# Routing to experts between the products of a graph network's last pass

## The chip, the cores and the metric

The program runs on one core of one Trainium2 chip. The metric is the device time of one execution in microseconds (us). Its engines have short names throughout: PE is TensorE's matmuls and PEld its weight loads, DVE is VectorE, ACT is ScalarE, POOL is GpSimd and SP is SyncE, which here only issues DMAs (SPq is its queue). Engines run their own instruction streams in order and wait for each other on semaphores.

## The reference, cut to what matters

The network has four layers over 3125 nodes of 256 features and 50000 edges. Each layer adds to `x` a graph part and a mixing part of the normed `x`, and then a feed-forward part. The change is in the fourth layer (number 3):

```python
xn = _layernorm(x)
x = x + gcn(xn, edges) + linear_attention(xn)      # gcn: three convolutions
# feed-forward of layer 3: 8 experts, each node goes to 2 of them
xt = _layernorm(x)
probs = softmax(xt @ Wr + br)
top_p, top_idx = top_k(probs, 2);  weights = top_p / top_p.sum(-1)
xe = norm(xt) * ln_g[e] + ln_b[e]                  # a second norm, affine by expert
y  = gelu(xe @ W1[e] + b1[e]) @ W2[e] + b2[e]      # 256 -> 1024 -> 256
x  = x + sum over the two experts of weights * y
```

One convolution is `agg[dst] += h[src] * norm`, then a bias. The third (512 to 256 features) ends with the sum over neighbours that finishes `x` for the feed-forward part.

## The kernel before, in words

**Tiles.** Nodes lie in `NB` = 25 blocks of 128 rows; `x` stays in SBUF. Where work goes by groups, a group is `BB` = 5 blocks. The program is written with a tile framework: Python calls record instructions, the framework gives tiles their buffers and every instruction its semaphore waits, and it may move an instruction that depends on nothing nearby to an earlier place. Pools are opened and closed; a tile in a pool opened later may lie where a closed pool lay, and then waits for that pool's readers.

**Layer 3's graph part.** `layer3` (L2294) reads a number and takes one of two branches of the program: `gcn3`, by gathers, or `dense3` (L2103), which this input takes. `dense3` does the sum over neighbours as a matrix product with a matrix of edge counts, one block of destinations at a time: `product(h, d)` (matmuls L2134) loads the 128 x 3200 bf16 counts of block `d` (0.8 MB, tile `a`, three buffers, by SP) and runs 75 matmuls of 128x256 (25 blocks of sources by three bf16 parts that make up an f32 value) into the PSUM tile `dn`, which has two buffers. Four passes of 25 products make the three convolutions (the second has 512 features, so two passes). In the last pass (L2219 to L2223) each product is followed by a single DVE instruction (L2222) that scales it and adds it to `x[:, d, :]`. When it has run for a block, that block of `x` is final for the feed-forward part. The PSUM pool of `dense3`, `ps`, has three buffers by default; besides `dn` it holds tiles called `mm`.

**The feed-forward part.** `ffn3` (L2305) calls `ffn` (L1726), which calls `mixture` (L1306), shared by layers 0, 1 and 3. `mixture` makes its tiles and returns two functions:

- `route(b)` (L1333 to L1395) for the group that starts at block `b`. Statistics of five blocks (`stats`, L435: on DVE the statistics L441 and L442 and the reciprocal L445, on ACT a square root L444), then for each block the norm on DVE (`normed`, L448), two transposes on PE and a copy out of PSUM on ACT or DVE (`to_T`, L451), and two matmuls per k for the 8 logits (`tok`, L459; an f32 matmul is two rows in the profile). Then a second norm into `xs`; the bias, the exponential, the softmax's division and the choice of two (`exps` L1543, `over_sum` L1553, `top2` L1565: DVE, with one ACT instruction). Two small matmuls over the group's choices count for each node how many earlier nodes went to the same expert; `run`, carried from group to group, adds the counts of earlier groups. DVE makes row numbers of them (L1368 and after), and POOL issues ten indirect DMAs (L1389) that scatter the five blocks of `xs` to `sent`, a DRAM table sorted by expert.
- `rest()` (L1397 to L1541) opens the pool of weights, loads `w2` of all experts (L1402, 8 issues of 1 MB by SP), works out on DVE which expert each of `ES` = 56 slots of 128 rows belongs to, and then runs the slots: for each SP loads the routed block `xr` (L1462), that expert's `w1` (L1464) and bias `br` (L1466); PE transposes and multiplies (`h`, L1494; `y`, L1507) with a Gelu on ACT between (L1498), and POOL scatters the result back (L1511). A last loop (L1538) adds both results of each node to `x`.

`ffn` calls `route` for the five groups one after the other, and then `rest`. All of this stands behind the join of the two branches. `mixture` also splits the experts' second bias `b2` into three bf16 parts and stores them in DRAM (`split3`, L1291: a load and a store by SP, five small instructions on DVE).

**What sets the order around the change.** Each engine runs in the order in which the framework placed the instructions, which is for the most part the order of the Python calls. In the last pass that is product after product; on SP, the loads of `a`, three products ahead at most. The branches of `layer3` are blocks of their own: nothing of the feed-forward part that uses `x` can stand ahead of the join.

Of the kernel before, what the change touches and what calls it, by code (L numbers as in the profile page):

```python
# [19 lines left out]
P = 128  # L20
N = 3125
D = 256
# [42 lines left out]
class Net:  # L65
# [484 lines left out]
    def gather_sum(self, pool, ps, table, w, agg, weighted=False, steps=None):  # L550
# [4 lines left out]
        for g in range(NS // G):  # L555
            msg = []
            for j in range(G):
                if j % n == 0:
                    m = pool.tile([P, n, w], F32, name="msg", bufs=7)
                self.gather(m[:, j % n, :], table, g * G + j)  # L560
                msg.append(m[:, j % n, :])
# [744 lines left out]
    def mixture(self, whole, mark, pre, names, kind, gate, gate_b, H, act, twice=False, affine=None):  # L1306


        nc, tc, a = self.nc, self.tc, self.a
# [10 lines left out]
        head = whole.enter_context(ExitStack())  # L1320
        r1 = head.enter_context(self.pool("ro", 1, side="right"))
        r = head.enter_context(self.pool("ro2", 2, side="right"))
        ps = head.enter_context(self.pool("ro_ps", 2, PSUM))

        xs = r1.tile([P, NB, DX], F32, name="xs")
        nc.vector.tensor_copy(xs[:, :, D:D + 2], self.goes)
        wg = self.weight(r1, gate)
        bg = self.rows(r1, gate_b[0])
        for nm in gate_b[1:]:
            nc.vector.tensor_add(bg, bg, self.rows(r1, nm))  # L1330
        b2d = self.split3(r, a[b2n].rearrange("e h -> (e h)"), NE * D, pre + "b2_3")

        def route(b):  # L1333
            mv, rs = self.stats(r, lambda i: self.x[:, b + i, :], BB, "ln")
            q = ps.tile([P, BB, NE], F32, name="lg", bufs=1)
            rows = xs[:, b:b + BB, :D]
            xn = r.tile([P, BB, D], F32, name="xn") if twice else rows
            for i in range(BB):
                self.normed(xn[:, i, :], self.x[:, b + i, :], mv, rs, i)
                xg = r.tile([P, 2, P], F32, name="xg", bufs=4)  # L1340
                self.to_T(ps, xn[:, i, :], xg)
                self.tok(q[:, i, :], xg, 0, wg)
# [15 lines left out]
            if kind != "plain":  # L1358
                self.over_sum(r, c, guard=b + BB == NB)

            q = ps.tile([P, 2, BB, NE], F32, name="rk", bufs=1)
# [24 lines left out]
            for i in range(BB):  # L1386
                n = LAST if b + i == NB - 1 else P
                for k in range(2):
# [4 lines left out]
                    if b + i + k:  # L1393
                        tc.declare_no_dep(s.ins, group=pre, reason="every row has a place of its own")
                    tc.add_to_no_dep_group(pre, s.ins)  # L1395

        def rest():  # L1397
# [3 lines left out]
            for e in range(NE):  # L1401
# [3 lines left out]
            w1d = a[w1n].rearrange("e d f -> (e d) f")  # L1405

            ni = r1.tile([P, NE], I32, name="ni")
            nc.vector.tensor_scalar(ni, run, 127.0, None, op0=ALU.add)
            nc.vector.tensor_scalar(ni, ni, 7, None, op0=ALU.logical_shift_right)
            nf = r1.tile([P, NE], F32, name="nf")  # L1410
            nc.vector.tensor_copy(nf, ni)
            zero = r1.tile([P, NE], F32, name="zero")
            nc.vector.memset(zero, 0.0)
            st = r1.tile([P, NE], F32, name="st")
            nc.vector.tensor_tensor_scan(st, nf, zero, 0.0, ALU.add, ALU.add)
            nc.vector.tensor_sub(st, st, nf)
            sl = r1.tile([1, ES], F32, name="sl")
            nc.gpsimd.iota(sl, pattern=[[1, ES]], base=0, channel_multiplier=0,  # L1418
                           allow_small_or_imprecise_dtypes=True)
            ex = r1.tile([1, ES], F32, name="exf")  # L1420
            nc.vector.memset(ex, 0.0)
            st0 = r1.tile([1, ES], F32, name="st0")
            nc.vector.memset(st0, 0.0)
            for e in range(1, NE):
                s = st[0:1, e:e + 1]
                nc.vector.scalar_tensor_tensor(ex, sl, s, ex, op0=ALU.is_ge, op1=ALU.add)
                t = r.tile([1, ES], F32, name="stt")
                nc.vector.tensor_scalar(t, sl, s, s, op0=ALU.is_ge, op1=ALU.mult)
                nc.vector.tensor_tensor(st0, st0, t, ALU.max)
            nc.vector.tensor_sub(sl, sl, st0)  # L1430

            place = r1.tile([1, ES], F32, name="place")
            nc.vector.tensor_scalar(place, sl, float(P), None, op0=ALU.mult)
            nc.vector.scalar_tensor_tensor(place, ex, float(NP), place, op0=ALU.mult, op1=ALU.add)
            q = ps.tile([P, ES], F32, name="own", bufs=1)
            nc.tensor.matmul(q, self.ones[0:1, :], place, start=True, stop=True)
            own, void = (p.tile([P, ES], F32, name=n) for n in ("own", "void"))
            nc.vector.tensor_scalar(own, q, self.row, float(1 + mark), op0=ALU.add, op1=ALU.add)
            nc.vector.tensor_scalar(void, q, self.row, float(2 * NP), op0=ALU.add, op1=ALU.add)
            nc.vector.tensor_scalar(sl, sl, float(NB - 1), float(P), op0=ALU.min, op1=ALU.mult)  # L1440
            exi = p.tile([1, ES], I32, name="exi")
            nc.vector.tensor_copy(exi, ex)
            rows_at = p.tile([1, ES], I32, name="rows_at")
            nc.vector.scalar_tensor_tensor(rows_at, ex, float(NP), sl, op0=ALU.mult, op1=ALU.add)
            head.close()
# [95 lines left out]
        return route, rest  # L1541
# [39 lines left out]
    def layer0(self):  # L1581
        with ExitStack() as whole:
            rest = []

            def after():
                route, r = self.mixture(whole, 0, "L0_ffn_", ("W1", "b1", "W2", "b2"), "plain", "L0_ffn_gate_w",
                                        ["L0_ffn_gate_b"], 512, AF.Gelu)
                rest.append(r)
                return route
# [15 lines left out]
            rest[0]()  # L1605
# [120 lines left out]
    def ffn(self, *args, **more):  # L1726
        with ExitStack() as whole:
            route, rest = self.mixture(whole, *args, **more)
            for b in range(0, NB, BB):
                route(b)  # L1730
            rest()

    def ffn1(self):
        self.ffn(1, "L1_ffn_", ("W1", "b1", "W2", "b2"), "chosen", "L1_ffn_Wg", ["L1_ffn_bg", "L1_ffn_bias"], 512, AF.Relu)
# [368 lines left out]
    def dense3(self):  # L2103
# [4 lines left out]
        with self.pool("dense", 1) as gw, self.pool("counted", 3) as ap, self.pool("dense2", 2) as gp, \  # L2108
# [69 lines left out]
            with self.pool("late", 1) as lw:  # L2178
# [33 lines left out]
                for half, h in enumerate((hb, ha)):  # L2212
                    for d in range(NB + 2):
# [4 lines left out]
                        if half and d >= 2 and ((d - 2) % 4 == 3 or d - 2 == NB - 1):  # L2218
                            wide((d - 2) // 4)  # L2219
                for d in range(NB):  # L2220
                    q = product(hb, d)
                    nc.vector.scalar_tensor_tensor(self.x[:, d, :], q, di[:, d:d + 1], self.x[:, d, :],  # L2222
                                                   op0=ALU.mult, op1=ALU.add)  # L2223

    def gcn3(self):
        nc, tc = self.nc, self.tc
        with self.pool("gnn", 1) as gw, self.pool("gnn2", 2) as gp:
# [18 lines left out]
            with self.pool("ps3", 2, PSUM) as ps, self.pool("mix", 1) as mw, \  # L2246
# [5 lines left out]
                self.gather_sum(gp, ps, tabs[0], D, half, steps=steps)  # L2252
# [11 lines left out]
                self.gather_sum(gp, ps, tabs[1], 512, agg, steps=steps)  # L2264
# [22 lines left out]
                self.gather_sum(gp, ps, tabs[2], D, half, steps=steps)  # L2287
# [6 lines left out]
    def layer3(self):  # L2294
        nc, tc = self.nc, self.tc
        unfit = nc.values_load(self.gathers[0:1, 0:1], min_val=0, max_val=3 * P,
                               skip_runtime_bounds_check_because="a count of rows, in three ways")
# [112 lines left out]
```

## Time and profile before

| what | value |
|---|---|
| time, median of 3 runs | 6230.42 us (6222.06 to 6235.17) |
| the profiled execution's own time | 6871.84 us |
| its span | 6870.1 us |
| mean granted clock of TensorE in it | 0.825 |
| busy in the span | PE 4752.5, DVE 3279.0, POOL 2383.8, ACT 1573.9 us |
| layer 3's last pass over destinations | 6067 to 6272 us |
| its routes | 6272 to 6400 us |
| its expert slots | from 6400 us to about 6830 us |

The profile is one execution on the chip; the hardware's profiler makes it longer than the executions that are timed, by 641 us here. Times inside it are given from the start of the span. PE is busiest, but no engine is busy all the time: the share of each is an average over many stages. In a row of the timeline the columns are the start, the duration, the engine with its source line, the operation, the tiles (written from read), the shapes, how many were put together, and in brackets how long the engine had been idle and what ended that. In the table by windows, PEclk is the mean clock that was granted to TensorE, as a share of full speed.

### The profile page before, as it was taken

Reading aid. Unit: us, or ns where it says so; the run is one execution under the profiler, and the core shown is the slowest. Engines: PE = TensorE matmul, PEld = TensorE weight load, DVE = VectorE, ACT = ScalarE, POOL = GpSimd, SP = SyncE. Lnnn points to the kernel's source line nnn. Section 1 sums busy time; section 2 is a strip of 40 time slices with the busy share of each in tenths; the row PEclk is TensorE's granted clock in tenths of the full one; section 3 lists DMA queues with packets and bytes.
Section 4 is the critical chain, followed back from the end, with each engine's and each line's share of the span. In section 5 each row is a group of like instructions: output and inputs, shape, how many; then the busy total and the mean of one; then the engine's idle time right before and its main releaser. Section 6 shows DMA issues by size and latency. Waiting matters only on the chain.

```text
span 6870.1 us, 81944 instructions
## 1 busy us (share of the span) xinstructions
PE 4752.5 (69%) x25310; PEld 3363.4 (49%) x25310; DVE 3279.0 (48%) x8628; ACT 1573.9 (23%) x4113; POOL 2383.8 (35%) x2340
## 2 busy tenths in 40 slices
PE   2375776396575556555577756777169999997797
PEld 1012344284454434433366313444046788786696
DVE  5146676634687537775534346667533200113222
ACT  1012223322100034442222112221124311101222
POOL 1605776321665534445231625665110000001211
PEclk9677888598787777777688877888589999997898
DMA  3362333264222223333155322333111232123454
GB/s 106 85 179 66 107 107 102 83 199 118 86 84 74 71 76 116 116 109 102 53 167 173 90 79 83 102 107 94 37 55 62 72 135 87 58 78 113 171 175 160
DMA packets 385094, 710.59 MB, mean 103 GB/s; under 512 B 100817, under 2 KB 223256, under 8 KB 384652
## 3 DMA queue, kind: packets, MB, share of 16 engines
q1 hardware_dynamic: 266431, 425.79, 20.0%
q0 software_dynamic: 108064, 269.63, 13.6%
q10 hardware_dynamic: 10157, 9.80, 0.4%
q8 instruction: 213, 3.49, 0.2%
q14 instruction: 229, 1.88, 0.1%
HBM read 571.51 MB, written 133.47 MB: 103 GB/s over the span
## 4 chain that ended last, share of the span: by engine, by line
PE 46%; issue 17%; DVE 15%; another core or an unknown queue 8%; DMA 5%; POOL 4%; ACT 3%; DVEq 2%; ACTq 1%; SPq 0%; POOLq 0%
PE dn L2134 12%; PE mm L465 6%; PE g L862 5%; PE g L585 3%; DVE agg L544 3%; PE y L1507 3%; PE h L1494 2%; DVE ohd L2065 2%; PE q L657 1%; PE q L666 1%; DMA terms<-outr 1%; PE mm L502 1%; DVEq L527 1%; PE mm L2194 1%
## 5 line engine op out<-in xcount | busy, mean ns | idle before, releaser
L531 POOL DMA_INDIRECT msg<-L_gnn_c_tab,src x832 | 820.0, 986 | 857.4 <-PE g L585 236.2
L531 POOL DMA_INDIRECT msg<-L_gnn_htab,src x832 | 893.7, 1074 | 588.6 <-issue 225.2
L544 DVE TENSOR_TENSOR agg<-agg,g 128x256 f32 (+2 forms) x1664 | 697.1, 419 | 588.6 <-remote 283.5
L2134 PEld LDWEIGHTS <-a 128*128 128x128 bf16 x7500 | 735.0, 98 | 118.1 <-issue 30.2
L862 PE MATMUL g<-msg,oh 128*128 128x261 f32 (+1 forms) x1664 | 591.8, 463 | 248.7 <-DVE agg L544 114.2
L585 PE MATMUL g<-msg,oh 128*128 128x256 f32 x1664 | 565.9, 489 | 229.0 <-DVE oh L566 138.7
L862 PEld LDWEIGHTS g<-msg,oh 128*128 128x128 f32 x1664 | 324.0, 218 | 510.3 <-issue 213.7
L585 PEld LDWEIGHTS g<-msg,oh 128*128 128x128 f32 x1664 | 387.7, 249 | 345.9 <-DVE oh L566 156.4
L1494 PE MATMUL h<-xe,w 128*128 128x128 f32 x3584 | 435.6, 278 | 7.3 <-DMA w<-in_L_ffn_W 7.3
L2134 PE MATMUL dn<-ha,a 128*128 128x256 bf16 x3750 | 426.2, 274 | 9.3 <-ACT ha L2119 7.8
L1511 POOL DMA_INDIRECT back<-y,toi x168 | 163.2, 971 | 773.4 <-DVE y L1510 537.9
L1507 PE MATMUL y<-w,hT 128*128 x1792 | 431.2, 388 | 0.0
L1494 PEld LDWEIGHTS h<-xe,w 128*128 128x128 f32 x3584 | 421.1, 194 | 8.7 <-issue 8.3
L2134 PE MATMUL dn<-hb,a 128*128 128x256 bf16 x3750 | 413.6, 273 | 0.0
L1498 ACT ACTIVATE hT<-h,br 128x128 f32<-128x128 f32 x896 | 256.3, 369 | 661.0 <-issue 572.7
L1418 POOL IOTA sl<- 1x56 f32 x3 | 0.5, 171 | 1123.7 <-PE dn L2134 1023.8
L1507 PEld LDWEIGHTS y<-w,hT 128*128 128x128 f32 x1792 | 326.5, 190 | 57.0
L1510 DVE COPY y<-y 128x256 f32<-128x256 f32 x168 | 71.2, 424 | 574.6 <-PE y L1507 574.4
L819 ACT COPY stage<-dm 128x24 bf16 (+1 forms) x832 | 182.7, 221 | 578.9 <-PE pd L825 193.5
L657 PE MATMUL q<-ohl,t 128*104 128x512 bf16 (+1 forms) x702 | 204.1, 423 | 126.3 <-issue 69.7
L1389 POOL DMA_INDIRECT sent<-xs,ids x150 | 154.8, 1032 | 355.9 <-DVE run L1368 189.2
L531 POOL DMA_INDIRECT ase<-tab,src x208 | 219.1, 1054 | 151.7 <-PE q L657 85.7
(724 smaller groups left out, 7619.8 us busy)
## 6 DMA issues: line engine op xcount, KB each, us to landing
a<-counted SPq DMA_DIRECT2D x100, 800.0 KB
w<-in_L_ffn_W SPq DMA_DIRECT2D x128, 512.0 KB
w<-in_L_ffn_W SPq DMA_DIRECT2D x64, 1024.0 KB
counted<-T SPq DMA_DIRECT2D x40, 800.0 KB
dr<-dl_rows SPq DMA_DIRECT2D x104, 256.0 KB
sent<-zeros SPq DMA_DIRECT2D x25, 1040.0 KB
xr<-sent SPq DMA_DIRECT2D x168, 130.0 KB
lw<-lo_rows SPq DMA_DIRECT2D x78, 256.0 KB
```

The source lines that it names most:

```text
L465: nc.tensor.matmul(q, xT[:, k, t * P:(t + 1) * P], w[:, k, cols], start=(k == 0 and bias is None), stop=(k == nk - 1))
L531: self.nc.gpsimd.indirect_dma_start(out=out, out_offset=None, in_=table, in_offset=bass.IndirectOffsetOnAxis(ap=self.src[:, t:t + 1], axis=0))
L544: self.nc.vector.tensor_tensor(at, at, q, ALU.add)
L585: self.nc.tensor.matmul(r, oh[:, j, :], msg[j], start=True, stop=True)
L657: nc.tensor.matmul(q[:M], t3[:, k, i, :], oh[:, k, :], start=((k, i) == mm[0]), stop=((k, i) == mm[-1]))
L819: nc.scalar.copy(rows[:, j, :], dmf[:, bass.ds(at, 6 * H)])
L862: nc.tensor.matmul(q, oh[:, j, :], msg[:, j, :], start=True, stop=True)
L1494: nc.tensor.matmul(q[:, i, :], d["w1"][:, k, c * P:(c + 1) * P], d["xe"][:, k, :], start=(k == 0), stop=(k == 1))
L1498: nc.scalar.activation(hT[:, c, :], q[:, i, :], act, bias=d["br"][:, c:c + 1])
L1507: nc.tensor.matmul(q, d["hT"][:, c, :], w2f[:, bass.ds(e * (nh * D) + c * D, D)], start=False, stop=(c == nh - 1))
L1511: s = nc.gpsimd.indirect_dma_start(out=self.back, out_offset=bass.IndirectOffsetOnAxis(ap=d["to"][:, 0:1], axis=0), in_=y, in_offset=None)
L2134: nc.tensor.matmul(q, a[:, k, :], h[:, k, i, :], start=(k == 0 and i == 0), stop=(k == NB - 1 and i == 2))
```

## The change

`mixture` now returns three functions. `begin` opens the pools of the routes and makes their tiles (`xs`, the gate's weight and bias), with either its own PSUM pools or that of its caller. `route` is a generator: it stops (`yield`) after the first norms and again after the choice of two, ahead of the counts. `rest` keeps its work, with its small tiles in the pool `p`, which stays open.

`layer3` is a generator too: it makes the mixture first and stops; goes on to the branches, and stops again; `rest` comes last. The branch of `dense3` makes the routes inside its last pass: after each product's addition to `x` one step of the open route is made, and after every fifth product the route of the five finished blocks is opened and runs to its first stop (statistics and first norms). So a group's transposes, logits and choice are recorded behind the first product of the next group, and its counts and scatters behind the second; what is left of the last group after the last product is recorded in one piece. Layer 1 and the branch `gcn3` make all routes in one piece as before (`routes`), and layer 0 exhausts each route where it called it. The split of `b2` goes to the pool `p`, and in layer 3 into the part ahead of the first stop. In `gcn3`, which doesn't run here, gathers are six ahead instead of seven.

```diff
-        b2d = self.split3(r, a[b2n].rearrange("e h -> (e h)"), NE * D, pre + "b2_3")
+        b2d = self.split3(p, a[b2n].rearrange("e h -> (e h)"), NE * D, pre + "b2_3")
+        has = {}
+        def begin(own, ps=None):
+            r1 = own.enter_context(self.pool("ro", 1, side="right"))
+            r = own.enter_context(self.pool("ro2", 2, side="right"))
+            few = ps
+            if ps is None:
+                few = own.enter_context(self.pool("ro_ps", 1, PSUM))
+                ps = own.enter_context(self.pool("ro_ps2", 2, PSUM))
...
         def route(b):
+            r1, r, few, ps, xs, wg, bg, group = has["now"]
             mv, rs = self.stats(r, lambda i: self.x[:, b + i, :], BB, "ln")
-            q = ps.tile([P, BB, NE], F32, name="lg", bufs=1)
+            q = few.tile([P, 512], F32, name="mm")[:, :BB * NE].rearrange("p (i e) -> p i e", e=NE)
...
             for i in range(BB):
                 self.normed(xn[:, i, :], self.x[:, b + i, :], mv, rs, i)
+            yield
+            for i in range(BB):
                 xg = r.tile([P, 2, P], F32, name="xg", bufs=4)
...
                 self.over_sum(r, c, guard=b + BB == NB)
+            yield
...
-        return route, rest
+        return begin, route, rest
```

In `rest`, the tiles from `ni` to `place` move from `r1` and `r` to `p`, and `head.close()`, which closed the routes' pools behind them, is gone: the caller closes them. The loops:

```diff
+    def routes(self, begin, route):
+        with ExitStack() as head:
+            begin(head)
             for b in range(0, NB, BB):
-                route(b)
-            rest()
+                for _ in route(b):
+                    pass
...
+            with ExitStack() as head:
+                begin(head, ps)
+                routes = []
                 for d in range(NB):
                     q = product(hb, d)
                     nc.vector.scalar_tensor_tensor(self.x[:, d, :], q, di[:, d:d + 1], self.x[:, d, :],
                                                    op0=ALU.mult, op1=ALU.add)
+                    for r in routes:
+                        next(r, None)
+                    if d % BB == BB - 1:
+                        routes = [route(d - BB + 1)]
+                        next(routes[0])
+                for r in routes:
+                    for _ in r:
+                        pass
...
     def layer3(self):
+        with ExitStack() as whole:
+            begin, route, rest = self.mixture(whole, 2, "L3_ffn_", ("W1", "b1", "W2", "b2"), "again", "L3_ffn_Wr",
+                                              ["L3_ffn_br"], 1024, AF.Gelu, twice=True, affine=("ln_g", "ln_b"))
+            yield
...
+                self.routes(begin, route)
         with cmp.Else():
-            self.dense3()
+            self.dense3(begin, route)
+            self.xT = None
+            yield
+            rest()
```

## The prediction

> **What bounds the kernel now.** I first read the page's busy tenths: TensorE (PE) is full over the last 1700 us except for one dip, and the clock row dips with it.
>
> ```profile
> PE   2375776396575556555577756777169999997797
> ...
> PEclk9677888598787777777688877888589999997898
> ```
>
> Each digit is 171.8 us. Slices 31 to 36 of PE are 9s, then come two 7s: about 6183 to 6527 us. The chain of waits shows what lies there, and the busy time by stages gives its size.
>
> ```profile
> 6067.56 204.37 PE dn L2134 x1872
> ...
> 6327.73 10.78 another core or an unknown queue
> 6388.65 25.54 issue
> ```
>
> ```profile
> core 0: us, PE busy (x) PEld busy (x) DVE busy (x) ACT busy (x) POOL busy (x), PEclk, DMA share, GB/s
> 6067.00:6272.00 205.00, 204.92 (x1875) 183.33 (x1873) 12.97 (x28) 1.21 (x3) 0.17 (x1) 1.00 0.27 89
> 6272.00:6400.00 128.00, 40.04 (x176) 35.51 (x176) 78.05 (x408) 25.43 (x49) 50.74 (x50) 0.51 0.39 128
> 6400.00:6830.00 430.00, 429.88 (x2852) 390.86 (x2852) 91.88 (x330) 129.40 (x449) 53.35 (x55) 0.99 0.50 169
> ```
>
> The pass of 25 products is PE alone, with VectorE (DVE) busy 13 of 205 us, ACT 1, POOL 0.2. Then the routes take 128 us, in which no engine is full and the PE clock is 0.51. Then the experts are PE alone again. So 128 us of many small waits lie between two stages that PE fills, while the first of them leaves every other engine free. The timeline gives the marks:
>
> ```profile
> 6271.96 0.48 DVE L2222 SCALAR_TENSOR_TENSOR x<-dn,di,x 128x256 f32<-128x256 f32 x1 [7.70 <-PE dn L2134]
> ...
> 6277.43 17.62 SPq L1402 DMA_DIRECT2D w<-in_L_ffn_W  x8
> ...
> 6387.09 1.56 POOL L1389 DMA_INDIRECT sent<-xs,ids  x1 [0.30 <-issue]
> ...
> 6394.29 0.37 SPq L1462 DMA_DIRECT2D xr<-sent  x1
> ...
> 6400.12 2.90 PE L1494 MATMUL h<-xe,w 128*128 128x128 f32 x12 [2.76 <-DMA w<-in_L_ffn_W]
> ```
>
> From the last product's end (call it T0, 6271.95) to the first expert product is 128.2 us. Within it the second expert weights w2 (8 MB) are loaded and nobody notices.
>
> **Part by part.** *Removed from the end:* the routes of groups 0 to 3 (blocks 0 to 19), which now run in steps between products. What is left behind T0 is the route of group 4, whose blocks 20 to 24 are complete only then.
>
> *The tail that stays,* from the rows of the last group in the routes' timeline. x update 0.48, statistics 0.40, aggregate 0.17, square root 0.30, reciprocal 0.18, and the handovers between them, some 0.1 each: 2.0. The first normed block (0.41): 2.4. From its transpose to the last logits 6349.37 to 6358.38, 9.0, less a 2.5 us pause of ACT: 8.9. Logits to the choice of two, 6359.77 to 6367.03: 16.3 with the handover. Rank products to row numbers, 6367.08 to 6371.35: 20.6. DVE ends its part 0.8 later: 21.4. Ten scatters on POOL, 6374.99 to 6388.65, 13.7 (1.27 apart): 34.5. Last scatter to the load of the first routed block, 6388.65 to 6394.29, 5.6: 40.1. That load to the first expert product, 5.8: **45.9 us**.
>
> *A new wait.* In the changed program's order the load of w2 stands after the join of the two branches, and waits for DVE's last count in the branch. Before, that followed the last x update; now it follows DVE's part of group 4, at 21.4. I take 22.4 for the issue. Data: in the DMA row of 6060 to 6420 us (9 us each) the three slices from 6276 carry 233, 348 and 347 GB/s, 8.4 MB, done at 6303, 25.6 after the issue. So w2 lands at 48.0, behind the 45.9. The routed block, w1 and biases stand behind w2 on SP's queue. Here a rule speaks against the change: the Trainium skill ("DMA: Bandwidth & Descriptors", Queues, rings and completion order) says that each DMA engine consumes one queue's descriptors in ring order. No run here shows a transfer behind w2. By the rule the first w1 (1 MB, 3.0 us at 347 GB/s, and 1.9 more as before: 4.9 from issue to use) follows the routed block (0.4): 53.3. If it overtook, 45.9. No row speaks for overtaking, so I take **53**. So 128 − 53 = 75 us leave the end.
>
> *Added to the pass.* A product here is 75 matmul rows. Per block two transposes and four logits rows. Transposes between products stand in the timeline of 6020 to 6050 us: 6023.58, next product row 6023.80, so 0.22 for two. The logits rows load 128x128 f32 weights like the expert products, 32 in 3.74 us: 0.117 each, 0.47. Five blocks 3.4, four rank rows 0.5: 3.9 per group, 15.5 for four. Waits of PE for the copies out of PSUM: a pair of transposes ends 0.38 after its start, the copy takes 0.37; in the changed order four product rows (0.109 each, 0.44) and fewer stand between, so about 0.4 per group is open. Sum **17**. It can't be below 15.5, since these rows are PE's own; above, the pace of the routes at clock 0.51, 1.17 per block and 1.1 for the rank, gives 28. The clock decides, and beside products it is 1.00, so the low end. A rule would have more: "TensorE: Matmul & The Clock Gate" (Part 4: PE-mode transpose) puts a transpose at about 275 ns and says that it doesn't raise the clock. Forty at 0.275 are 11.0 against 4.4, so 24. The row (0.11 each, at clock 1.00) decides.
>
> *Behind waiting instructions.* PE waits for the choice of two before the rank products, and product rows queue behind. From logits to choice 7.3 less the second norm (5 x 0.41, earlier in the changed order) is 5.2; the order puts 64 product rows (7.0 us) between. Wait 0; without that cover 5 per group. On DVE the x update of a product queues behind a step of the route, at most five norms twice and five statistics, about 7 us; the accumulator has two buffers, so 8.2 us of slack. Cost 0; if a step took over 8.2, PE would stand for the rest.
>
> *Queues.* POOL's 40 scatters land in a stage where it had 0.2 us of work, 5.3 MB more in 205 us at DMA share 0.27: 0. SP gets the gate's two loads among the products' loads, which have three buffers: 0. The bias split (a load and a store on SP, five small casts on DVE, 0.1 to 0.2 each) moves to the start of layer 2: in the changed order its casts stand on DVE behind the last statistics there and ahead of the last group's reciprocal. Before, the reciprocal (3774.13) idled 0.38 for ACT, and the chain of waits runs through the norms behind it. So 0.9 less 0.38, some 0.5, if the load is there, as its neighbours' (issued at 3752.9) were; up to 4.5, its whole way from load to store in before, if DVE waits for it; below 0 nothing. Its store stands on SP ahead of the mix weights (3777.44), which come later anyway. I take 0.5. In layers 0 and 1 the chain of expert numbers has one buffer less; it ended at 6380.4, 8 us before the scatters here. 0, either way at most 2.
>
> *Sum.* 75 − 17 − 0.5 = 57.5, say 58 us off the profiled execution (span 6870.1, 6871.8 in all): 6814. The median is 6230.4; profiling adds 10%, and I can't see where. Some 14 us of the gap (the 10.8 and shorter pauses) have no cause in the trace. I scale, 58 x 0.907 = 53: **6177 us**.
>
> **Rivals.** *(A) As above,* 6160 to 6192: PE's addition between 15.5 and 28 (minus 11), the tail between 46 and 53 (plus 7), scaled, and the unexplained pauses either way. 0.66. *(B) The load of w2 takes the place of the routes.* If it waits for the last scatter too (40.1) the tail is 40 + 26 + 5 = 71, and the gain 128 − 71 − 17 = 40, scaled 36: 6194; with pauses of 14 in the tail, 6207. For it: the load waits on counts of all queues at the join. Against: by the order, DVE's is the last of them. 0.16. *(C) Slower: PE's in-order queue.* If the steps stood without cover, PE would wait 16.3 us before each of four ranks, 65, and with the 17 that eats the 75 and 7 more; each gap also drops the clock. After the gap at 6400 the first 20 rows took 0.16 instead of 0.117 for some 6 us, about 3 us lost; two gaps in each of four groups make 24. Together +31, scaled +28: 6258. It decides from 14.6 us of PE idling per group (58/4). Against: the 64 product rows in the order. 0.06. *(D) It doesn't do what it says:* scheduling puts most steps behind the last product, or other layers lose what this gains: within 12 us of 6230. Against: the changed order shows four groups in the products. 0.06. *(E) More:* w1 overtakes w2 and nothing is scaled, 128 − 46 − 15.5 = 66, with other pauses gone 80: 6150 to 6160. 0.06.
>
> **How the numbers follow.** A is likeliest, 6177. The range 6150 to 6212 takes in A, B and E, and leaves C and D out. About 0.2% (12.5 us) is what a measurement can tell from no change. Faster by more: A, B and E, 0.88; within: D, 0.06; slower: C, 0.06.
>
> **What would show it.** In the changed profile: the pass of last products grows from 204.5 to about 221 us with the clock at 1.00, and PE's idling in it under 3 us; between the last product and the first expert product some 53 us; w2's first issue some 22 us behind the last product, and the first expert product ended by DMA. Wrong: long PE waits for the choice or the copies in the pass (C), w2 issued only behind the scatters (B), or a tail well under 50 (E).

## The result and the profile after

The changed kernel takes 6191.19 us (median of 4 runs, 6183.65 to 6196.5) against 6230.18 for the kernel before: a ratio of 0.9936, 95% interval 0.992 to 0.9951, so 39 us less (30 to 50). The forecast was 53 less. Its profiled execution took 6189.69 us, with a span of 6187.9, no longer than its other runs: profiling adds nothing. So the first profile of before, 6871.84 us, isn't an execution of 6230 us that the profiler made longer. The runs below have the same program at about 6240 us on some chips (the short kind) and at 6816 to 6887 on others (the long kind), where the profiles have pauses for which no row gives a cause. The first profile looks like the long kind, though the record doesn't name its chip. Every ratio below compares kernels on one chip.

Line numbers are from here on those of the changed kernel: the product L2154, w2's load L1415, the scatters L1402, the load of `b2` L1461, the routed block L1475, w1 L1477. Its page, PE and its clock in 40 slices of 154.7 us:

```profile
PE   1848775696778766656697758880699999997997
...
PEclk9969887797897777777798879995899999998998
```

Where before had two slices of 7 there is one (slice 37, 5569 to 5724 us, has it), and what is left of the dip ends at 5718. The windows of the changed kernel give pass, stretch between the last product and the first expert product, and experts:

```profile
core 0: us, PE busy (x) PEld busy (x) DVE busy (x) ACT busy (x) POOL busy (x), PEclk, DMA share, GB/s
5443.30:5664.10 220.80, 220.16 (x2009) 196.68 (x2007) 83.77 (x324) 22.07 (x40) 38.99 (x40) 1.00 0.32 107
5664.10:5718.10 54.00, 8.21 (x41) 6.48 (x41) 24.04 (x106) 3.78 (x9) 10.90 (x10) 0.55 0.67 215
5718.10:6148.00 429.90, 429.88 (x2850) 391.14 (x2851) 92.51 (x330) 129.41 (x449) 53.50 (x55) 0.99 0.49 168
```

PE has 136 rows more in the pass than before, still fills it at clock 1.00, and DVE, ACT and POOL now work beside it. The waits of PE in the pass come to 0.4 us. The stretch is 54.0 us, and the experts take what they took (431.4 us from the first product to the start of the last scatter back, 430.8 before). Its timeline has the marks of the new tail:

```profile
5664.15 0.48 DVE L2245 SCALAR_TENSOR_TENSOR x<-dn,di,x 128x256 f32<-128x256 f32 x1 [7.03 <-PE dn L2154]
...
5683.42 0.20 DVE L1398 TENSOR_REDUCE cw<-e 128x5 f32<-128x40 f32 x1
5683.82 22.25 SPq L1415 DMA_DIRECT2D w<-in_L_ffn_W  x8
...
5695.24 1.56 POOL L1402 DMA_INDIRECT sent<-xs,ids  x1 [0.30 <-issue]
...
5706.44 2.51 SPq L1461 DMA_DIRECT2D b<-L_ffn_b  x1
5709.74 0.37 SPq L1475 DMA_DIRECT2D xr<-sent  x1
5710.63 0.39 SPq L1477 DMA_DIRECT2D w<-in_L_ffn_W  x1
...
5718.12 3.32 PE L1507 MATMUL h<-xe,w 128*128 128x128 f32 x14 [1.50 <-DMA w<-in_L_ffn_W]
```

Read with T0 = 5664.1, the end of the last product: DVE ends its part at 19.5, SP starts on w2 at 19.7 and is busy issuing it until 42.0, though the last scatter ended at 32.7; the routed block follows at 45.6, w1 at 46.5, the first expert product at 54.0. In the chain of waits of the changed kernel the same stretch is SP's, where before it was the routes':

```profile
5703.16 2.91 SPq L1415
...
5706.44 2.51 SPq L1461
...
5710.63 7.36 DMA w<-in_L_ffn_W
...
5718.12 3.32 PE h L1507 x14
```

### The profile page after: what moved, and what is told of

It reads as the page before. It is cut to its first block, busy times and chain, and to the rows that moved or that the text cites. A ratio compares the mean times of both kernels' runs of the same rounds, so it can differ in the third digit from the quotient of the medians.

```text
span 6187.9 us, 81932 instructions
## 1 busy us (share of the span) xinstructions
PE 4643.9 (75%) x25310; PEld 3283.6 (53%) x25310; DVE 3297.2 (53%) x8633; ACT 1567.8 (25%) x4108; POOL 2397.0 (39%) x2340
## 4 chain that ended last, share of the span: by engine, by line
PE 43%; issue 17%; DVE 15%; POOL 11%; DMA 8%; ACT 3%; DVEq 2%; SPq 1%; ACTq 0%; another core or an unknown queue 0%; POOLq 0%
PE dn L2154 13%; PE mm L465 6%; POOL msg L531 6%; PE g L585 4%; PE g L862 3%; DMA msg<-L_gnn_htab,src 2%; PE h L1507 2%; PE y L1520 2%; DVE ohd L2085 2%; POOL ase L531 2%; DVE agg L544 2%; DMA terms<-outr 2%; POOL back L1524 1%; PE mm L2214 1%; PE mm L2098 1%
## 5 line engine op out<-in xcount | busy, mean ns | idle before, releaser
L2154 PEld LDWEIGHTS <-a 128*128 128x128 bf16 x7500 | 736.2, 98 | 116.9 <-issue 28.3
L862 PE MATMUL g<-msg,oh 128*128 128x261 f32 (+1 forms) x1664 | 568.7, 450 | 194.0 <-DVE agg L544 176.5
L1402 POOL DMA_INDIRECT sent<-xs,ids x150 | 153.0, 1020 | 1292.9 <-DMA yb<-done,backs 1036.3
L585 PE MATMUL g<-msg,oh 128*128 128x256 f32 x1664 | 581.6, 484 | 86.5 <-DMA msg<-L_gnn_c_tab,src 35.5
L862 PEld LDWEIGHTS g<-msg,oh 128*128 128x128 f32 x1664 | 314.2, 211 | 433.6 <-DVE agg L544 328.2
L585 PEld LDWEIGHTS g<-msg,oh 128*128 128x128 f32 x1664 | 358.5, 238 | 235.4 <-DVE oh L566 86.8
L2154 PE MATMUL dn<-ha,a 128*128 128x256 bf16 x3750 | 428.5, 275 | 7.7 <-ACT ha L2139 6.5
L2154 PE MATMUL dn<-hb,a 128*128 128x256 bf16 x3750 | 418.2, 273 | 0.0
L851 DVE TENSOR_TENSOR msg<-msg,alpha 128x1024 f32<-128x1024 f32 x208 | 254.1, 1222 | 133.4 <-DMA msg<-L_gnn_htab,src 119.9
L531 POOL DMA_INDIRECT ase<-tab,src x208 | 231.8, 1115 | 148.4 <-PE q L657 85.3
L566 DVE TENSOR_SCALAR oh<-cols,dl,ew 128x128 f32<-128x128 f32 x832 | 266.6, 350 | 0.0
```

The costliest lines, as they stand in the source:

```text
L531: self.nc.gpsimd.indirect_dma_start(out=out, out_offset=None, in_=table, in_offset=bass.IndirectOffsetOnAxis(ap=self.src[:, t:t + 1], axis=0))
L566: nc.vector.tensor_scalar(oh[:, j, :], self.cols, self.dl[:, t:t + 1], self.ew[:, t:t + 1], op0=ALU.is_equal, op1=ALU.mult)
L585: self.nc.tensor.matmul(r, oh[:, j, :], msg[j], start=True, stop=True)
L851: nc.vector.tensor_tensor(mh, mh, bc(al_, [None, None, None, C]), ALU.mult)
L862: nc.tensor.matmul(q, oh[:, j, :], msg[:, j, :], start=True, stop=True)
L2154: nc.tensor.matmul(q, a[:, k, :], h[:, k, i, :], start=(k == 0 and i == 0), stop=(k == NB - 1 and i == 2))
```

## The experiments

Ratios are to the kernel before on the same chip, with their 95% intervals; pass and stretch are of one profile each. "Pass" is from the first to the last row of the last pass's products, "stretch" from there to the first expert product.

| kernel | ratio | pass | stretch | before's median there |
|---|---|---|---|---|
| before again | 0.9998 (0.9992 to 1.0005) | 204.5 | 117.1 | 6242.75 |
| all routes behind | 1.0001 (0.9993 to 1.0009) | 204.6 | 117.2 | 6242.75 |
| one eighth of w2 | 0.9913 (0.99 to 0.9927) | 220.9 | 45.1 | 6242.75 |
| no cover | 1.0018 (1.001 to 1.0026) | 274.5 | 54.5 | 6242.75 |
| experts in both branches | 0.9934 (0.9914 to 0.9954) | 248.8 | 45.0 | 6887.05 |
| the same, last group 3 + 2 | 0.9922 (0.9896 to 0.9948) | 249.8 | 35.4 | 6887.05 |
| last group 3 + 2 alone | 0.995 (0.9932 to 0.9969) | 249.5 | 48.4 | 6887.05 |
| w2 issued by ScalarE | 0.9954 (0.9927 to 0.9981) | 247.2 | 51.9 | 6887.05 |
| changed kernel again | 0.9958 (0.9938 to 0.9978) | 248.6 | 54.6 | 6878.54 |
| both branches, 3 + 2, again | 0.9928 (0.9899 to 0.9958) | 251.5 | 35.2 | 6878.54 |
| steps at once | 0.997 (0.995 to 0.9991) | 251.6 | 54.7 | 6878.54 |
| no scatters of four groups | 0.9948 (0.9922 to 0.9974) | 220.9 | 61.4 | 6815.89 |

**Before again.** The kernel before, unchanged.

> The kernel before, unchanged, for a second profile of it and a comparison with itself. My theory: the first profile of before was stretched by pauses without a cause in it (529 us over the span, 10.8 and some 3 of them between the last product and the first expert product), which timed runs don't have. Then this profile spans about 6230 us, and the stretch from last product to first expert product is 112 to 118 us instead of 128.2; the change is then worth 115 less 54 less 16, about 45. The rival, that profiling stretches every stage alike: a span near 6870, the stretch again 128. A third: a clean span but a stretch of 126 to 130, and then some 20 us of the gain are lost in another stage of the changed kernel. The ratio to before is 1.000, its interval shows what the comparison can tell.

Its profile spans 6231.7 us. Its chain, which here reaches back to 3524 us only, has no entry for "another core or an unknown queue". Its windows of pass and stretch are:

```profile
5440.10:5644.60 204.50, 204.50 (x1873) 183.06 (x1871) 12.93 (x27) 1.22 (x3) 0.17 (x1) 1.00 0.27 90
5644.60:5761.70 117.10, 39.45 (x176) 35.37 (x176) 77.49 (x408) 25.43 (x49) 51.05 (x50) 0.52 0.43 141
```

Busy times in the stretch are those of the first profile within 0.6 us (PE 39.45 against 40.04), but the stretch is 117.1 instead of 128.2. So 11.1 us of the 128.2 were pauses of that execution. With the change, pass and stretch together fall from 321.6 to 274.8 us, 46.8 less, and 39 (30 to 50) were measured: this speaks for the first theory. But that timed runs don't have such pauses is wrong as I put it: on three other chips the timed runs are as long as the first profile.

One thing that the pauses have in common I had overlooked. Of the waits for "another core or an unknown queue" in the first profile's chain, POOL is issuing indirect DMAs in each of the 27 longest, and is busy for 191 of their 280.6 us. An early stretch of before shows it, first in the first profile and then in the second:

```profile
222.00:360.00 138.00, 29.58 (x50) 6.74 (x50) 10.98 (x20) 5.75 (x10) 96.47 (x101) 0.56 0.22 51
```

```profile
222.00:360.00 138.00, 107.62 (x280) 27.21 (x280) 63.44 (x122) 30.25 (x56) 98.08 (x103) 0.89 0.79 202
```

POOL goes on at its pace (101 against 103 rows), while PE, DVE and ACT are busy less than a third as long. The pause of 10.8 us in the stretch, too, lies beside scatters, the last seven of the second group's ten. That is a coincidence in the traces; the last experiment takes scatters away.

**All routes behind the last product.** In the changed kernel:

```diff
-                    for r in routes:
-                        next(r, None)
-                    if d % BB == BB - 1:
-                        routes = [route(d - BB + 1)]
-                        next(routes[0])
-                for r in routes:
-                    for _ in r:
-                        pass
+                for b in range(0, NB, BB):
+                    for _ in route(b):
+                        pass
```

> The changed kernel, but with the five routes one after the other behind the last product, so that only the moved tiles, pools and the moved bias split remain of the change. My theory: the pass of last products is back at 204.5 us, the stretch to the first expert product at 115 or a few more (w2 waits for the end of all routes now, which adds up to 15), so 6230 to 6245. The rival, that the rebuilt pools and the moved split cost or save something in the earlier layers: over 0.2% away from that, with the difference ahead of layer 3's last pass.

Pass and stretch are those of before, and so is the time. The rebuilt pools, the moved small tiles and the moved bias split therefore cost nothing that can be measured (0.09% at most, 6 us); the gain is in the interleaving. The 15 us that I had allowed for w2 don't appear: w2 isn't issued before 83 us behind the last product, but the routes themselves end 9 us earlier (last scatter over at 96.0 instead of 105.2).

**One eighth of w2.**

```diff
-            for e in range(NE):
+            for e in range(1 if twice else NE):
...
-                        nc.tensor.matmul(q, d["hT"][:, c, :], w2f[:, bass.ds(e * (nh * D) + c * D, D)],
+                        nc.tensor.matmul(q, d["hT"][:, c, :], w2f[:, c * D:(c + 1) * D] if twice else w2f[:, bass.ds(e * (nh * D) + c * D, D)],
```

> The changed kernel, which loads only the first expert's second weights in layer 3 and uses them for every expert (seven of eight loads are left out). My theory: behind the last product SP is busy issuing w2 for 22 us and the loads of the first slot stand behind it; without that the last scatter decides, and the first expert product comes 41 to 46 us behind the last product instead of 54: 6178 to 6183. The rival, that the chain of the last group's route and scatters sets the end anyway: 54 us, 6191.

The timeline of this kernel, T0 at 5673.2:

```profile
5693.68 0.38 SPq L1415 DMA_DIRECT2D w<-in_L_ffn_W  x1
...
5705.09 1.55 POOL L1402 DMA_INDIRECT sent<-xs,ids  x1 [0.30 <-issue]
...
5711.30 0.26 SPq L1461 DMA_DIRECT2D b<-L_ffn_b  x1
...
5713.22 0.39 SPq L1477 DMA_DIRECT2D w<-in_L_ffn_W  x1
```

With SP free, the bias load follows the last scatter by 4.7 us and the first expert product stands at 45.1, within 1 us of the 45.9 that the prediction gave the chain without w2. So w2 is the new wait, and 9 us of the tail are its own.

**No cover.** Each group's route is recorded in one piece behind its fifth product, and the next product is made to wait for the group's choice, through a zero that is added to `hb`, which that product reads:

```diff
-            yield
+            yield sel
...
-                    for r in routes:
+                    if d % BB == BB - 1:
+                        r = route(d - BB + 1)
+                        next(r)
+                        sel = next(r)
+                        if d < NB - 1:
+                            zero = gw.tile([P, 1], F32, name="zero")
+                            nc.vector.tensor_scalar(zero, sel[:, 0, 0:1], 0.0, None, op0=ALU.mult)
+                            nc.vector.tensor_scalar(hb[:, 0, 0, :], hb[:, 0, 0, :], zero, None, op0=ALU.add)
                         next(r, None)
-                    if d % BB == BB - 1:
-                        routes = [route(d - BB + 1)]
-                        next(routes[0])
```

> The changed kernel with the cover taken away: after each of the first four routes' choices a zero made of the choice is added to one piece of hb, so the next product's first row waits for the choice (the sum is not changed by it). The rival of the prediction that ends slower: PE stands about 16 us, less its own 4, behind each of four groups, 48 to 65, and up to 24 more for rows at a lower clock: 6240 to 6280, no faster than before. My theory of the gain expects the same of this edit, and that the pass of last products grows from 221 to 270 to 310 with most of the wait on DVE; if the time stays near 6191, the cover is not what the gain rests on.

Its windows, and what PE waited for in the pass (sum, times, longest):

```profile
5443.20:5717.70 274.50, 238.15 (x2009) 210.26 (x2007) 82.08 (x328) 22.89 (x44) 38.88 (x40) 0.89 0.26 86
```

```profile
PE mm L1376 <- DVE sel L1590: 24.0, 4, 6.0
PE mm L456 <- DVE xn L449: 9.3, 4, 2.4
PE mm L465 <- ACT xg L457: 2.9, 7, 0.5
```

The pass is 53.7 us longer than the changed kernel's: 36.2 of waits, 9 per group, and 18.0 because the same rows take 238.15 us instead of 220.16 at a clock of 0.89. The change is then slower than before. Its gain rests on the cover, as the rival said. (The recording in one piece is not what costs: "Steps at once" below has it without the zero.)

**Where w2 is issued.** The experts' part recorded in each branch, so that no join stands ahead of w2:

```diff
-        def rest():
+        def rest(whole=whole):
...
                 self.routes(begin, route)
+                with ExitStack() as own:
+                    rest(own)
             with cmp.Else():
                 self.dense3(begin, route)
+                with ExitStack() as own:
+                    rest(own)
...
-            rest()
```

> The changed kernel, but the experts' part is recorded inside each of the two branches instead of once behind their join, so that w2's load no longer waits for the end of VectorE's part of the branch, only for the memory it goes to. My theory of the new wait: w2 is issued some 2 to 4 us behind the last product instead of 20, SP is done with it at about 25, and the last scatter (33) decides again: first expert product 45 us behind the last product as with one eighth of w2, about 9 us less than the changed kernel, ratio near 0.992. The rival, that w2's 8 MB in the way of the scatters costs as much as its early start saves: 52 to 56 us, ratio 0.9935.

w2 is issued 0.6 us behind T0 instead of 19.7, has landed before the last scatter, and the stretch is 45.0: again the scatters' chain, with all of w2 loaded. The join cost 9.6 us (54.6 on such a chip). The ratio alone, 0.9914 to 0.9954, can't tell this; the trace does.

**The last group in three and two blocks.** `route` takes the number of blocks (every `BB` in it becomes `nb`), and

```diff
-                    if d % BB == BB - 1:
-                        routes = [route(d - BB + 1)]
+                    if d in ends:
+                        routes = [route(d - ends[d] + 1, ends[d])]
```

with `ends = {4: 5, 9: 5, 14: 5, 19: 5, 22: 3, 24: 2}`. Alone, with w2 behind the join:

> The changed kernel with the last group divided in three and two blocks, and w2 behind the join as it was. My theory: w2's load follows the end of VectorE's part, which comes 4 to 6 us earlier (14 to 16 us behind the last product), and the 34 us from its issue to the first expert product stay: 48 to 50 us instead of 54, ratio 0.993. If the scatters were what decides, taking six of them (7.6 us) and the shorter row work off would give 42.

48.4: w2 is issued 15.3 us behind the last product, 4.4 earlier, and the rest is as long as ever. The last scatter is over at 20.7 and decides nothing. With the experts in both branches:

> As rest_twice, and the last group of five blocks is divided in a group of three (routed between products too) and one of two, so that 4 scatters instead of 10 are left behind the last product. My theory: six scatters of 1.27 and the shorter row work of VectorE come off the chain, the last scatter ends 19 to 21 us behind the last product, then SP's issue of w2 (done at about 25) and its data (28) decide: first expert product at 33 to 36 us, 18 to 21 us less than the changed kernel, ratio 0.990. The rival, that the chain is latency of small instructions whatever the group's size: 42 us or more.

35.4. The timeline of this kernel, T0 at 6327.1:

```profile
6327.63 20.06 SPq L1415 DMA_DIRECT2D w<-in_L_ffn_W  x8
...
6346.11 1.55 POOL L1402 DMA_INDIRECT sent<-xs,ids  x1 [0.30 <-issue]
...
6355.23 0.27 SPq L1461 DMA_DIRECT2D b<-L_ffn_b  x1
...
6357.17 0.39 SPq L1477 DMA_DIRECT2D w<-in_L_ffn_W  x1
```

SP is done with w2 at 20.6, as the last scatter ends; the bias load, ahead of which SP waits for the scatters to land, comes 7.6 us later, not 4.7 as where w2 was out of the way. Both edits are needed, and neither gives its whole worth alone.

**w2 issued by ScalarE.**

```diff
-                nc.sync.dma_start(w2[:, e, :].rearrange("p (k f) -> p k f", k=nh),
+                (nc.scalar if twice else nc.sync).dma_start(w2[:, e, :].rearrange("p (k f) -> p k f", k=nh),
```

> The changed kernel with w2's eight loads of layer 3 issued by ScalarE instead of SP. It tells whether the first slot's loads are late because SP is busy issuing w2 for 22 us, or because their data queue behind w2's. If the issue: b2, the routed block and w1 are issued by 40 us behind the last product and the first expert product comes at 45 to 48. If the data's order or bandwidth: they are issued early but land late, and the first expert product stays at 52 to 55, with w1 taking 10 us or more from issue to use. I lean to the issue for the routed block, and some delay of w1.

The timeline of this kernel, T0 at 6324.6:

```profile
6345.35 22.47 ACTq L1415 DMA_DIRECT2D w<-in_L_ffn_W  x8
...
6365.95 0.26 SPq L1461 DMA_DIRECT2D b<-L_ffn_b  x1
...
6368.15 0.39 SPq L1477 DMA_DIRECT2D w<-in_L_ffn_W  x1
```

Mostly the data. SP was free, but the bias load came 7.5 us behind the last scatter, and w1 took 8.3 us from issue to use (5.6 with w2 landed, 7.5 in the changed kernel): 51.9, only 2 to 3 us better. So w1 is late behind w2 on another queue too.

**The changed kernel again, and the best one.**

> The changed kernel again, on the chip of the next two. The kernel before took 6887 us on one chip and 6243 on another, so the change's worth is to be read beside before on one chip. My theory: 47 us by the traces of both kernels (321.7 less 274.8 from the start of the last pass to the first expert product), a ratio of 0.9925; if the first comparison's 0.9936 is right to its last digit, some 7 us are lost elsewhere.

> The experts' part recorded in both branches and the last group divided in three and two blocks, again, beside the changed kernel on one chip. My theory: the first expert product 35 us behind the last product as in its first profile, 18 to 19 us less than the changed kernel, 0.3%: a ratio to before of 0.9895 to 0.991. If something behind the first product gave it back (w1 and the routed blocks late while w2 lands), no more than 0.1% apart from the changed kernel.

The best version's stretch is 35.2 again, 19.4 shorter than the changed kernel's; pass and stretch together are 16.5 us less, 0.24% of 6879, and the ratios differ by 0.3%. It was run only on chips of the long kind, where its two ratios lie below the changed kernel's, with intervals that overlap. The ratios that I expected of both were too low, because on this chip the pass had grown to 248.6 us:

```profile
6087.10:6335.70 248.60, 232.90 (x2009) 200.47 (x2007) 83.76 (x324) 22.06 (x40) 38.96 (x40) 0.95 0.28 95
```

PE is busy 12.7 us longer and idle 15.7 instead of 0.6. The timeline of the same run shows where PE stood, beside the first group's scatters (and in the same place beside those of the next three):

```profile
6153.41 1.01 POOL L1402 DMA_INDIRECT sent<-xs,ids  x1 [1032.57 <-DMA yb<-done,backs]
...
6163.45 0.49 PE L2154 MATMUL dn<-hb,a 128*128 128x256 bf16 x3 [0.86 <-issue]
...
6163.69 0.97 POOL L1402 DMA_INDIRECT sent<-xs,ids  x1 [0.30 <-issue]
6164.88 0.38 PE L2154 MATMUL dn<-hb,a 128*128 128x256 bf16 x2 [0.94 <-issue]
...
6164.97 0.97 POOL L1402 DMA_INDIRECT sent<-xs,ids  x1 [0.30 <-issue]
6165.61 0.27 PE L2154 MATMUL dn<-hb,a 128*128 128x256 bf16 x1 [0.35 <-issue]
```

The product rows stand still in pieces of 0.2 to 1.5 us, with "issue" as the only reason, beside the last four of a group's ten scatters and until 2 us behind them. Before, no scatter ran in this pass, and it took 204.4 us in the first profile, the only one of before with such pauses. If before's stretch is as long here as there, the change gains 332.6 (204.4 and 128.2) less 303.2 (248.6 and 54.6), 29.4 us or 0.43%, and 0.42% was measured.

**Steps at once.** Each route recorded in one piece behind its fifth product:

```diff
-                    for r in routes:
-                        next(r, None)
                     if d % BB == BB - 1:
-                        routes = [route(d - BB + 1)]
-                        next(routes[0])
+                        for _ in route(d - BB + 1):
+                            pass
```

> The changed kernel without the two stops: each group's route is recorded in one piece behind its fifth product. By the placed order its PE rows are still spread between the product rows of the next product, since the framework places them by its own estimate. My theory: what covers the choice is that placing, not the stops, so the pass stays at 219 to 224 us and the time within 0.1% of the changed kernel. The rival, that the stops give the cover: PE waits for copies and choices in the pass, 4 to 10 us per group, 16 to 40 in all.

The pass takes 251.6 us, 3.0 more than the changed kernel's beside it (the 219 to 224 that I wrote are for a chip without pauses), and the ratios differ by 0.12%, which their intervals can't tell apart. The 3 us are waits of PE for the choice, 3.0 us in the four groups, which the changed kernel doesn't have. So the two stops are worth about this much of the pass, and the cover comes for the most part from the framework's own placing.

**No scatters of the first four groups.**

```diff
-            for i in range(BB):
+            for i in range(BB if b + BB == NB or not twice else 0):
...
-                    if b + i + k:
+                    if (i + k if twice else b + i + k):
```

The second pair gives the first scatter that is left the place in the framework's order that the very first had.

> The changed kernel without the 40 scatters of the first four groups in layer 3 (their rows are left out of the experts' table, so the last layer's output lacks them; the amount of the experts' work stays). On a chip where before takes near 6880 us, the last pass took 248.6 us with the change, not 220.8: 16.8 us of PE's pauses, all but a few in the second half of a group's ten scatters or just behind it, and a lower clock behind them. My theory: the scatters bring these pauses; without them the pass is at 219 to 223 us on such a chip too, 28 us less than with them, a ratio to before of 0.991 to 0.993. The rival, that the pauses come with the product rows and the routes' other steps: the pass stays near 248. On a chip where before takes near 6240 us, the pass is 221 either way and the run tells only that the scatters cost the pass nothing there.

```profile
5989.80:6210.70 220.90, 220.19 (x2009) 196.66 (x2007) 83.61 (x325) 22.06 (x40) 0.00 (x0) 1.00 0.25 83
6210.70:6272.10 61.40, 9.11 (x40) 7.28 (x40) 22.93 (x106) 3.88 (x9) 10.94 (x10) 0.53 0.60 191
```

The pass is back at 220.9 on a chip of the long kind, with 0.4 us of PE waits: without the scatters there are no pauses in it. It was another such chip than those where the pass took 247 to 252, and the changed kernel was not run there, so this holds as far as one chip of the long kind stands for another. The stretch grew to 61.4, since by the chain w2 now stands behind a landed scatter of the last group: it is issued 28.1 us behind the last product. Pass and stretch together are 50.3 us less than before's 332.6, 0.74%, which lies within the ratio's wide interval (0.26 to 0.78%).

## Why the prediction was right, and what was mis-sized

**The mechanism held.** The routes of four groups left the end, PE paid for their rows in the pass, and w2 behind DVE's part of the branch became the wait that ends last. Rival B's longer wait didn't come in the change itself; the run without scatters shows that it was close: there w2 did wait for a scatter.

**The pass.** Forecast 17 us, measured 16.3. The rows cost 15.7 (220.16 less 204.50 of busy time, forecast 15.5), the copies out of PSUM 0.4 in all (forecast 0.4 per group). The clock stayed at 1.00, so the row of 0.11 us per transpose was right where the rule would have given 24. The trace shows how both figures can hold: each of the 40 transpose rows lasts 0.273 us, about what the rule says (there for bf16, here for f32), but the next row starts 0.11 us behind it. The rule's figure is how long one row lasts, not what it costs in a row of them.

**The tail.** Forecast 53, measured 54.0, by a somewhat different way. DVE ended at 19.5 instead of 21.4 and w2 was issued at 19.7 instead of 22.4. SP then took 22.25 us for the eight issues instead of 17.6, so the routed block came at 45.6, behind SP's issuing, where the forecast had it at 48.0, behind w2's data; and w1 took 7.5 us to its use instead of 4.9. That the sum is right within 1 us is in part luck: the two misses, 2.4 and 2.6 us, go against each other. The chain without w2, forecast 45.9, measured 45.1 and 45.0. That w1 doesn't overtake w2 was right; but the order of one queue can't be the whole reason, since w1 was late behind w2 on ScalarE's queue too (51.9).

**The step that was mis-sized** is the stretch before: "128 − 53 = 75 us leave the end". Of the 128.2 us 11.1 were pauses of an execution that is 10% longer as a whole; the clean stretch is 117.1. The prediction had named "some 14 us of the gap" without a cause and then scaled the whole gain by 0.907 (58 to 53). A uniform scale was the wrong correction: neither the pass (204.4 and 204.5) nor the experts (430.8 and 430.2 from the first product to the start of the last scatter back) differ between the two profiles of before. The pauses lie elsewhere, and 11 us of them in this stretch. That 53 is nearer to what was measured than 58 is luck: the scale took off 5 us for the wrong reason. Taking the pauses out and scaling nothing gives 117.1 − 54.0 − 16.3 = 46.8 and 6183; 6191 (6184 to 6197) was measured. Whether the last 7.8 us are noise or a loss can't be told from the intervals. The work ahead of the last pass is no steadier than that: it ends at 5443.3 us in the changed kernel's profile, and on one chip at 5443.2 without cover, 5452.4 with all routes behind and 5452.4 with one eighth of w2, with the same code there. Across the runs the change in pass and stretch together gives every ratio within its interval (46.8 us are 0.75%, 0.49 to 0.80 measured), where before's sum is 321.6 on the one kind of chip and, from the first profile, 332.6 on the other.

**What was costed at nothing.** The bias split, forecast 0.5: from the last addition of layer 1 to layer 2's first product it is 24.96 us in before's second profile and 24.98 in the changed kernel's. Layers 0 and 1, forecast 0: all routes behind the last product gives 1.0001. POOL's 40 scatters, forecast 0: right on the chip of the result (0.4 us of PE waits), wrong by some 28 us on two of the others, where the scatters bring pauses. The first profile of before had a sign of it, the pause of 10.8 us beside the second group's scatters, which the prediction left without a cause.

**Rival C.** Its mechanism is real and its price was too high, by a double count. It put the wait before each of four ranks at 16.3 us. In the run without cover the product rows do stand 15.4 to 16.3 us apart at these places, but only 9 us of each are waits; the rest is PE's own rows of the route, which the forecast had in its 17 already. The lower clock was put at 24 and measured 18. Together 54 of the forecast 89, and still enough to make the change slower than before (1.0018). In rival E, 6230 less its 66 us is 6164, not 6160; nothing hangs on it.

## What to carry to other kernels

Work that leaves most engines free can be hidden in a stage that fills one engine, at the price of that engine's own rows, if no row placed there has to wait; take the cover away and the same edit loses. When a chain of small steps leaves the critical path, look for the load that used to be hidden in it: here the join held w2 back for 19 us (issued at 19.7 instead of 0.6), and only moving it and shortening the scatters together took the tail from 54 to 35. Compare a profile's span with the timed runs first. Where it is longer, find the stages in which the pauses lie and take them out there, or profile again, before a sum is scaled; and look what runs beside the pauses, since moving that work can move them too, as with the scatters here.

## What the runs showed of the hardware that was not expected

One program takes 6230 to 6243 us on some chips and 6816 to 6887 on others, with hardly another busy time in the stage studied here. In the profiles of the long kind some waits in the chain have no cause (7.7% of the span in the first profile), and in the 27 longest of them there POOL issues indirect DMAs. On two of these chips ten scatters on POOL went with PE's rows, which wait for no semaphore then, standing still in pieces of 0.2 to 1.6 us and with a lower clock (0.95 in the pass): some 28 us for 40 scatters, and none on a third such chip when the scatters were left out. That other indirect DMAs bring the other pauses is not shown, and what in the chip ties the two together stays open.

Issuing 8 MB by eight DMAs held SP for 17.8 us in before's second profile and for 18.0 with the experts in both branches, where it was over before the last group's scatters began, but for 22.3 in the changed kernel, with the scatters beside it.
